# A layer norm's reciprocal deviation moved from GpSimd to ScalarE, with its followers one slot earlier

## The chip, the cores and the metric

One NeuronCore of a Trainium2 chip runs the whole kernel. The metric is the device time of one execution in microseconds; for the kernel before it is 16218.26 us, the median of three runs (16214.16 to 16220.73). Below, PE is TensorE (matmuls), DVE is VectorE, ACT is ScalarE, POOL is GpSimd, and SP is the engine that issues the DMAs.

## The reference, cut to what matters

Two layers work on x of shape (2, 256, 256, 128), fp32, each on a group-normalised input and with a residual. Layer 0 is an attention over rows. Layer 1, which takes nearly all of the time, is a selective scan (a state-space layer) over the L = 65536 pixels of each image, with 256 inner channels and 16 states:

```python
xi, z = split(x @ in_proj_w.T)
xs = silu(depthwise_conv3x3(xi) + conv_b)
dts, Bs, Cs = split(x_proj_w @ xs)
delta = softplus(dt_w @ dts + dt_b)
# for each channel d and state n, along the pixels l:
h[d,n,l] = exp(delta[d,l] * A[d,n]) * h[d,n,l-1] + delta[d,l] * xs[d,l] * Bs[n,l]
y[d,l]   = sum_n h[d,n,l] * Cs[n,l] + Ds[d] * xs[d,l]
mu  = y.mean(over d);  var = ((y - mu)**2).mean(over d)
y   = (y - mu) * rsqrt(var + 1e-5) * ln_g + ln_b
out = x + (y * silu(z)) @ out_proj_w.T
```

The change concerns the rsqrt(var + 1e-5) of the layer norm over the 256 channels, what follows from it, and the sum over n in y.

## The kernel before

**Tiling.** Layer 1 runs in 128 steps (2 images x 64). A step k covers R = 4 image rows, that is T = 1024 pixels. Partitions hold 32 channels times 4 states, so 256 channels and 16 states give 8 x 4 = 32 units a step, each a tile of 128 x 1024. A unit is (k, h, m, q): half h of the channels, group m of states, quarter q of the half.

**The order by hand.** The main loop (from L1041) counts slots t, one unit to a slot, 32 slots to a step; every engine but SP executes its instructions in exactly the order in which the loop emits them. In slot t stand, in this order:

- drive (L951, POOL, odd slots): hb = du * B for the pair of units t+3, t+4, one product of 128x2048
- products (L985, POOL, even slots): h * C for a pooled pair t-2, t-1. Pooled pairs begin at slots 2, 6, 10, 18 and 26 (L588, modulo 32)
- decay (L943, ACT): da = exp(delta * A) of unit t+1, into one of two PSUM tiles
- scan (L964, DVE): the recurrence over the 1024 pixels, from da, hb and the state; for a pooled unit the result goes to hb, otherwise back to da
- product (L976, DVE): h * C into the tile yc, only for units that are not pooled
- y_out (L1024, ACT): copies the finished sum y from PSUM to ys, for the half whose last group of states starts at unit t-8
- the pieces that other parts have put into the slot: those of project, which makes the inputs of a later step (convolution, gates, delta), and those of finish_row, which normalises one image row of an earlier step; first the ones for the other engines, then TensorE's. Within a slot, finish_row's pieces come ahead of project's
- add_up (L998, PE): sums four units over their states into the PSUM tile y, at slot t for units t-6 to t-3. It frees the two yc tiles (of four) that it read
- remember (L971, ACT): the last column of the scan becomes the state

Since ACT keeps this order, a decay can start only after all of the previous slot's ACT pieces and its remember.

**finish_row** (L802) begins at slot a, which is 8, 16, 24 or 0 modulo 32 for the four rows of a step. Its pieces, with their offsets from a before the change: turn (0, PE, y minus its mean, to pixels x channels), stats (1, ACT, squares with a running sum into lss), scales (2, POOL), norm (4, ACT, times rstd), back (5, PE, transposes), gated (6, DVE, yg), mix (7, PE), leave (8, ACT). scales therefore falls on slots 2, 10, 18 and 26, and it is two small GpSimd instructions: lve = lss / 256 + 1e-5 (L838), rstd = lve to the power -1/2 (L839).

**Pieces of project beside it on ACT**, modulo 32: states_out at slots 1 and 2 (L731), size_out at 3, 9, 10 and 11 (L747), softplus at 13 (L755), gate_out at 17, 18, 19 and 27 (L706), silu_z at 21 (L711), normalise at 25 and 26 (L657), silu_xs at 29 (L689). All matmul results of project share one PSUM bank (tag "p"), so each of its matmuls waits until ACT has emptied the last one.

Of the kernel before, what the change touches and what calls it, by code (L numbers as in the profile page):

```python
# [8 lines left out]
F32 = mybir.dt.float32  # L9
AF = mybir.ActivationFunctionType  # L10
ALU = mybir.AluOpType
# [4 lines left out]
P = 128  # L16
GN_EPS = 1e-5
LN_EPS = 1e-5
# [3 lines left out]
def attn_then_ssm_kernel(  # L22
# [26 lines left out]
    nc = tc.nc  # L49
# [4 lines left out]
    DI = in_proj_w.shape[0] // 2  # L54
# [8 lines left out]
    const = ctx.enter_context(tc.tile_pool(name="const", bufs=1))  # L63
# [18 lines left out]
    make_identity(nc, ident)  # L82
    ones_mean = const0.tile([P, P], F32, name="ones_mean")
    nc.vector.memset(ones_mean, 1.0 / P)
    neg_half = const.tile([P, TB // P], F32, name="neg_half")
    nc.vector.memset(neg_half, -0.5)

# [36 lines left out]
    NQ = P // CQ  # L124
    NCG = DI // CQ
    NSG = NS // SR
# [5 lines left out]
    with tc.tile_pool(name="prep", bufs=1) as prep, tc.tile_pool(  # L132
        name="prep2", bufs=3
# [120 lines left out]
    with tc.tile_pool(name="st", bufs=1) as stp, tc.tile_pool(  # L254
        name="st_x", bufs=6
# [20 lines left out]
    with ExitStack() as actx:  # L276
# [242 lines left out]
        end = B * NA  # L519
# [64 lines left out]
    WT = W // P  # L584
# [5 lines left out]
    s2 = ctx.enter_context(tc.tile_pool(name="s2", bufs=2))  # L590
# [14 lines left out]
    def at(t, piece, *args, pe=False):  # L605

        slots.setdefault(t, ([], []))[pe].append((piece, args))
# [194 lines left out]
    def finish_row(k, b, row, t0, a):  # L802
        o = {}

        def fetch():
            o["xres"] = s1.tile([P, WT, C], F32, name="xres")
            nc.sync.dma_start(
                out=o["xres"], in_=x1[b][row].rearrange("(t p) c -> p t c", p=P)
            )
            o["szr"] = s1.tile([P, NH, W], F32, name="szr")  # L810
            nc.sync.dma_start(
                out=o["szr"], in_=given[k]["sz"][:, :, t0 : t0 + W].rearrange("h p t -> p h t")
            )

        def turn():
            o["yt"] = ps_f.tile([P, WT, DI], F32, name="yt", tag="f")
            for j in range(WT):
                for h in range(NH):
                    nc.tensor.matmul(  # L819
                        o["yt"][:, j, :],  # L820
                        ys[k, h][:, t0 + j * P : t0 + (j + 1) * P],
                        centre[:, (1 - h) * P : (1 - h) * P + DI],
                        start=(h == 0),
                        stop=(h == NH - 1),
                    )

        def stats():
            yn = o["yn"] = s1.tile([P, WT, DI], F32, name="yn")
            o["ss"] = s2.tile([P, WT], F32, name="lss")
            for j in range(WT):  # L830
                nc.scalar.activation(  # L831
                    yn[:, j, :], o["yt"][:, j, :], AF.Square, accum_out=o["ss"][:, j : j + 1]
                )

        def scales():
            o["rstd"] = s2.tile([P, WT], F32, name="rstd")
            ve = s2.tile([P, WT], F32, name="lve")
            nc.gpsimd.tensor_scalar(ve, o["ss"], 1.0 / DI, LN_EPS, ALU.mult, ALU.add)  # L838
            nc.gpsimd.tensor_tensor(o["rstd"], ve, neg_half[:, 0:WT], ALU.pow)  # L839

        def norm():
            for j in range(WT):
                nc.scalar.activation(  # L843
                    o["yn"][:, j, :],
                    o["yt"][:, j, :],
                    AF.Copy,
                    scale=o["rstd"][:, j : j + 1],
                )

        def back():  # L850
            o["yd"] = ps_f.tile([P, NH, W], F32, name="yd", tag="f")
            for h in range(NH):
                for j in range(WT):
                    nc.tensor.transpose(  # L854
                        o["yd"][:, h, j * P : (j + 1) * P],
                        o["yn"][:, j, h * P : (h + 1) * P],
                        ident,
                    )

        def gated():  # L860
            o["yg"] = s1.tile([P, NH, W], F32, name="yg")
            nc.vector.tensor_tensor(o["yg"], o["yd"], o["szr"], ALU.mult)  # L862

        def mix():
            o["o"] = ps_f.tile([P, WT, C], F32, name="o1_ps", tag="f")
            nc.tensor.matmul(o["o"], ident, o["xres"], start=True, stop=False)  # L866
            for j in range(WT):
                for h in range(NH):
                    for i, by in enumerate(("yg", "szr")):
                        nc.tensor.matmul(  # L870
                            o["o"][:, j, :],
                            o[by][:, h, j * P : (j + 1) * P],
                            w_out[:, i, h, :],
                            start=False,
                            stop=(j == WT - 1 and h == NH - 1 and i == 1),
                        )

        def leave():
            ob = s1.tile([P, WT, C], F32, name="ob")
            nc.scalar.copy(ob, o["o"])  # L880
            nc.sync.dma_start(
                out=out_tok[b, row * W : (row + 1) * W, :].rearrange("(t p) c -> p t c", p=P),
                in_=ob,
            )

        at(a, fetch)
        for i, piece in (
            (0, turn),
            (1, stats),
            (2, scales),  # L890
            (4, norm),
            (5, back),
            (6, gated),
            (7, mix),
            (8, leave),
        ):
            at(a + i, piece, pe=piece in (turn, back, mix))
# [5 lines left out]
    def unit(t):  # L903

        k, i = divmod(t, NU)
        h, i = divmod(i, NM)
        m, q = divmod(i, NQ)
        return k, h, m, q
# [31 lines left out]
    def pooled(t):  # L940
        return t % NU - t % 2 in POOLED
# [43 lines left out]
    def products(t):  # L985

        k, h, m, q = unit(t)
        hb = units[t]["pair"]
        yc = s4.tile([P, 2, T], F32, name="yc")
        for i in range(2):  # L990
            units[t + i]["yc"] = yc[:, i, :]
        nc.gpsimd.tensor_tensor(  # L992
            yc, hb, repeats["cc", k, h, m].unsqueeze(1).to_broadcast([P, 2, T]), ALU.mult
        )
# [3 lines left out]
    def add_up(t):  # L998

        k, h, m, _ = unit(t)  # L1000
        if m == 0:
            xr = s1.tile([P, T], F32, name="xr")
            nc.sync.dma_start(out=xr, in_=given[k]["xs"][h])
            y = outs["y"] = ps_y.tile([P, T], F32, name="y")
            for i in range(NB):
                cols = slice(i * TB, (i + 1) * TB)
                nc.tensor.matmul(
                    y[:, cols], d_diag[:, h, :], xr[:, cols], start=True, stop=False
                )
        y = outs["y"]  # L1010
        for i in range(NB):
            cols = slice(i * TB, (i + 1) * TB)
            for q in range(NQ):
                nc.tensor.matmul(  # L1014
                    y[q * CQ : (q + 1) * CQ, cols],
                    sel,
                    units[t + q]["yc"][:, cols],
                    start=False,
                    stop=(m == NSG - 1),
                )  # L1020
        for q in range(NQ):
            del units[t + q]

    def y_out(t):  # L1024
        k, h, _, _ = unit(t)
        ys[k, h] = s2.tile([P, T], F32, name=f"ys{h}")
        nc.scalar.copy(ys[k, h], outs["y"])
# [4 lines left out]
    end = len(steps) * NU  # L1032
# [7 lines left out]
    with tc.manual_schedule(engines=engines):  # L1040
        for t in range(min(slots), max(slots) + 1):  # L1041
            if 0 <= t + AHEAD < end:
                fetch(t + AHEAD)
            if 0 <= t < end and t % (NU * NSTEP) == 0:
                st = s1.tile([P, NCG, NSG], F32, name="state")
                nc.gpsimd.memset(st, 0.0)
                states_of[steps[t // NU][0]] = st
            if 0 <= t + 3 < end and t % 2:
                drive(t + 3)
            if 0 <= t - 2 < end and t % 2 == 0 and pooled(t - 2):  # L1050
                products(t - 2)
            if 0 <= t + 1 < end:
                decay(t + 1)
            if 0 <= t < end:
                scan(t)
                if not pooled(t):
                    product(t)
            if 0 <= t - 8 < end and unit(t - 8)[2:] == (NSG - 1, 0):
                y_out(t - 8)
            for pieces in slots.pop(t, ()):  # L1060
                for piece, args in pieces:
                    piece(*args)
            if 0 <= t - 6 < end and (t - 6) % NQ == 0:
                add_up(t - 6)
            if 0 <= t < end:
                remember(t)

# [36 lines left out]
```

## Time and profile before

| what | value | from |
|---|---|---|
| span | 16220.2 us | the page |
| layer 0 and set-up, until the first scans | about 2690 us | the first y sums start at 2697.4 us |
| DVE busy, 4000 to 16000 us | about 96.6% | 1932.80 us in the last 2000 of it |
| POOL busy, same stretch | 97.8% | 1955.10 us |
| ACT busy, same stretch | 68.4% | 1368.25 us |
| PE busy, same stretch | 85.2% | 1703.14 us |
| scan of 128x1024 (DVE) | 2.346 us | the group of L969 |
| product of 128x1024 (DVE) | 1.225 us | the group of L983 |
| decay of 128x1024 (ACT) | 1.117 us | the group of L947 |
| drive or products of 128x2048 (POOL) | 4.54 us | the groups of L957 and L992 |
| lve and rstd (POOL) | 0.191 and 0.689 us | the groups of L838 and L839 |
| table load (ACT) | 1.283 us | the groups of ACT_TABLE_LOAD |

How to read it: busy is the time in which an engine executed something, over a stretch. The busy shares of the whole span mix layer 0 with layer 1, so the stretch from 4000 to 16000 us, which is layer 1 alone, is the one to read. A row of a group gives the line, the engine and operation, the tile written and the tiles read, the shape, the count, the busy time with the mean of one in nanoseconds, and the idle time of that engine just ahead. A row of waits gives who waited for whom, the total in us, how often, and the longest. A row of the timeline gives the start, the duration, the engine, line and operation, and in brackets the idle time before it and what ended it. An ACT_TABLE_LOAD is an instruction of its own on ScalarE: it brings in the table that the next activation function needs.

### The profile page before, as it was taken

The page shows a single profiled execution, that of the slowest core. Times are in us where ns is not written, and L with a number is a line of the kernel's source. Part 1 is how long each engine was busy: PE and PEld are TensorE (multiplying, and loading weights), DVE is VectorE, ACT ScalarE, POOL GpSimd, SP SyncE. Part 2 cuts the span into 40 slices and gives each one's busy share as a digit, 9 for nine tenths or more (in the row PEclk, how much of TensorE's full clock was granted, in tenths as well). Part 3 has the DMA queues.
Part 4 walks back from the last instruction along what each step waited for, and adds up shares of the span by engine and source line. Part 5 has one row for each costly group of instructions (what it writes and reads, how often), then busy time and mean ns, then how long its engine had stood idle before and what let it go on. Part 6 is the DMA issues. An engine that isn't in the chain of part 4 may idle for free. (4 is left out here: it accounts for less than half of the span.)

```text
span 16220.2 us, 178642 instructions
## 1 busy us (share of the span) xinstructions
PE 14005.8 (86%) x59451; PEld 7034.3 (43%) x59451; DVE 14617.8 (90%) x12483; ACT 10627.5 (66%) x18973; POOL 13488.7 (83%) x4240
## 2 busy tenths in 40 slices
PE   6999997888888888888888888888888888888886
PEld 5877883333333333333333333333333333333333
DVE  7665555999999999999999999999999999999998
ACT  3555554666666666666666666666666666666665
POOL 1111114999999999999999999999999999999998
PEclk8999998999999999999999889999999999999998
DMA  4322223666666666666666666666666666666665
GB/s 184 129 95 79 94 79 133 236 235 242 233 234 236 237 236 236 242 234 231 238 235 237 233 234 230 238 235 234 241 233 231 238 234 238 237 240 236 228 239 180
DMA packets 1428911, 3452.16 MB, mean 213 GB/s; under 512 B 119784, under 2 KB 711184, under 8 KB 1407504
## 3 DMA queue, kind: packets, MB, share of 16 engines
q1 hardware_dynamic: 1427984, 3440.73, 59.0%
q8 instruction: 468, 7.67, 0.2%
q14 instruction: 459, 3.76, 0.1%
HBM read 2752.41 MB, written 687.88 MB: 212 GB/s over the span
## 5 line engine op out<-in xcount | busy, mean ns | idle before, releaser
L957 POOL TENSOR_TENSOR hb<-du_r,bb 128x2048 f32<-128x2048 f32 x2048 | 9266.3, 4542 | 71.3 <-DMA du_r<-du_d 15.4
L969 DVE TENSOR_TENSOR_SCAN da<-da,state,hb 128x1024 f32<-128x1024 f32 x2816 | 6607.3, 2346 | 164.7 <-ACT da L947 131.5
L947 ACT ACTIVATE da<-delta_r,a_neg 128x1024 f32<-128x1024 f32 x4096 | 4575.5, 1117 | 84.2 <-DMA delta_r<-delta_d 0.2
L670 PE MATMUL u_ps<-xn,w_tap 128*128 128x512 f32 x9216 | 4230.8, 604 | 7.3 <-ACT sz L706 3.4
L983 DVE TENSOR_TENSOR yc<-da,cc 128x1024 f32<-128x1024 f32 x2816 | 3449.3, 1225 | 423.5 <-PE y L1014 257.4
L969 DVE TENSOR_TENSOR_SCAN hb<-da,state,hb 128x1024 f32<-128x1024 f32 x1280 | 2946.7, 2335 | 15.9 <-ACT da L947 15.9
L992 POOL TENSOR_TENSOR yc<-hb,cc 128x2048 f32<-128x2048 f32 x640 | 2906.7, 4542 | 62.3 <-ACT delta L747 46.8
L670 PEld LDWEIGHTS u_ps<-xn,w_tap 128*128 128x128 f32 x9216 | 1699.1, 194 | 2438.7 <-issue 2003.2
L1014 PE MATMUL y<-yc,sel 128*32 128x512 f32 x16384 | 2562.2, 752 | 14.8 <-POOL yc L992 14.8
L974 ACT COPY state<-da 128x1 f32<-128x1 f32 x2816 | 441.3, 157 | 2838.3 <-DVE yc L983 2797.8
L433 POOL TENSOR_TENSOR x1g<-xc,bo_all 128x512 f32<-128x512 f32 x256 | 315.7, 1272 | 1841.1 <-DVE stats L482 1839.2
L819 PE MATMUL yt<-centre,ys 128*128 128x256 f32 x4096 | 1037.6, 397 | 510.0 <-ACT ob L880 510.0
L695 PE MATMUL z_ps<-xn,w_z 128*128 128x512 f32 x1024 | 801.3, 875 | 696.1 <-ACT sz L706 424.0
L1014 PEld LDWEIGHTS y<-yc,sel 128*32 128x32 f32 x16384 | 492.5, 126 | 1942.6 <-issue 1703.9
L383 ACT ACTIVATE e<-s_ps,nmx 128x256 f32<-128x256 f32 x1024 | 477.0, 475 | 968.6 <-DVE nmx L374 939.9
L819 PEld LDWEIGHTS yt<-centre,ys 128*128 128x128 f32 x4096 | 744.6, 192 | 691.1 <-ACT ob L880 607.6
L736 PE MATMUL dt_ps<-xd,w_dt 8*128 8x512 f32 x1024 | 691.0, 759 | 350.9 <-ACT delta L747 233.2
L870 PE MATMUL o_ps<-w_out,szr 128*128 128x128 f32 x4096 | 797.7, 277 | 0.0
L870 PE MATMUL o_ps<-w_out,yg 128*128 128x128 f32 x4096 | 796.6, 276 | 0.0
L350 DVE TENSOR_TENSOR v<-v_ps,bv_all 128x512 f32<-128x512 f32 x256 | 177.0, 692 | 591.5 <-PE v_ps L343 591.5
L764 POOL TENSOR_TENSOR xs<-delta,xs 128x1024 f32<-128x1024 f32 x256 | 598.7, 2364 | 98.3 <-ACT delta L755 98.3
L870 PEld LDWEIGHTS o_ps<-w_out,yg 128*128 128x128 f32 x4096 | 666.9, 193 | 27.1
(132 smaller groups left out, 16764.6 us busy)
## 6 DMA issues: line engine op xcount, KB each, us to landing
bb<-bc_d SPq DMA_DIRECT2D x1024, 512.0 KB, 4.3
cc<-bc_d SPq DMA_DIRECT2D x1024, 512.0 KB, 4.4
delta_r<-delta_d SPq DMA_DIRECT2D x1024, 512.0 KB, 6.2
du_r<-du_d SPq DMA_DIRECT2D x1024, 512.0 KB, 6.1
sz_d<-sz SPq DMA_DIRECT2D x128, 1024.0 KB, 6.7
szr<-sz_d SPq DMA_DIRECT2D x512, 256.0 KB, 5.6
xs_d<-xs SPq DMA_DIRECT2D x128, 1024.0 KB, 6.6
xr<-xs_d SPq DMA_DIRECT2D x256, 512.0 KB, 5.0
```

Source lines behind the costliest of these rows:

```text
L670: nc.tensor.matmul(o["u"], w_tap[:, h, tap, :], xn[:, i * RB + dy : i * RB + dy + RB, dx : dx + W], start=(tap == 0), stop=(tap == 8),)
L695: nc.tensor.matmul(o["z"], w_z[:, h, :], xn[:, 1 + i * RB : 1 + (i + 1) * RB, 1 : W + 1], start=True, stop=True,)
L736: nc.tensor.matmul(o["dt"], w_dt[:, h, :], o["xd"][0:DR, i * TB : (i + 1) * TB], start=True, stop=True,)
L764: nc.gpsimd.tensor_tensor(du, o["delta"][:, h, :], du, ALU.mult)
L819: nc.tensor.matmul(o["yt"][:, j, :], ys[k, h][:, t0 + j * P : t0 + (j + 1) * P], centre[:, (1 - h) * P : (1 - h) * P + DI], start=(h == 0) ...
L870: nc.tensor.matmul(o["o"][:, j, :], o[by][:, h, j * P : (j + 1) * P], w_out[:, i, h, :], start=False, stop=(j == WT - 1 and h == NH - 1 an ...
L947: nc.scalar.activation(da, spreads["delta", k, h, q], AF.Exp, scale=a_neg[:, g, m : m + 1])
L957: nc.gpsimd.tensor_tensor(hb, spreads["pair", k, h, q], repeats["bb", k, h, m].unsqueeze(1).to_broadcast([P, 2, T]), ALU.mult,)
L969: nc.vector.tensor_tensor_scan(u["h"], u["da"], u["hb"], st, ALU.mult, ALU.add)
L983: nc.vector.tensor_tensor(u["yc"], u["h"], repeats["cc", k, h, m], ALU.mult)
L992: nc.gpsimd.tensor_tensor(yc, hb, repeats["cc", k, h, m].unsqueeze(1).to_broadcast([P, 2, T]), ALU.mult)
L1014: nc.tensor.matmul(y[q * CQ : (q + 1) * CQ, cols], sel, units[t + q]["yc"][:, cols], start=False, stop=(m == NSG - 1),)
```

## The change

The reciprocal deviation is now exp(-1/2 * ln(lss / 256 + 1e-5)), two activations on ScalarE in place of the two instructions on GpSimd. It is for taking the small work off GpSimd, which is nearly always busy, and for keeping the row's statistics on the engine that makes and uses them. Since rstd is then ready within its slot, norm and back come one slot earlier. y's sums come one slot earlier where all four units are DVE's, that is for units 12, 20 and 28 modulo 32; those of units 0, 4, 8, 16 and 24, with a pooled pair among them, stay. The copy of y to ys comes one slot earlier too, from slots 20 and 4 to 19 and 3.

```diff
+    ln_eps = const.tile([P, 1], F32, name="ln_eps")
+    nc.vector.memset(ln_eps, LN_EPS)
...
         def scales():
+            lv = s2.tile([P, WT], F32, name="lve")
+            nc.scalar.activation(lv, o["ss"], AF.Ln, bias=ln_eps, scale=1.0 / DI)
             o["rstd"] = s2.tile([P, WT], F32, name="rstd")
-            ve = s2.tile([P, WT], F32, name="lve")
-            nc.gpsimd.tensor_scalar(ve, o["ss"], 1.0 / DI, LN_EPS, ALU.mult, ALU.add)
-            nc.gpsimd.tensor_tensor(o["rstd"], ve, neg_half[:, 0:WT], ALU.pow)
+            nc.scalar.activation(o["rstd"], lv, AF.Exp, scale=-0.5)
...
-            (4, norm),
-            (5, back),
+            (3, norm),
+            (4, back),
...
-            if 0 <= t - 8 < end and unit(t - 8)[2:] == (NSG - 1, 0):
-                y_out(t - 8)
+            if 0 <= t - 7 < end and unit(t - 7)[2:] == (NSG - 1, 0):
+                y_out(t - 7)
...
-            if 0 <= t - 6 < end and (t - 6) % NQ == 0:
-                add_up(t - 6)
+            for u in (t - 6, t - 5):
+                if 0 <= u < end and u % NQ == 0 and (u == t - 6) == pooled(u + NQ - 1):
+                    add_up(u)
```

## The prediction

> **What bounds the kernel now.** I read the page's busy shares first, then who VectorE waits for in the steady stretch from 4000 to 16000 us, then the rows of one step in order of time.
>
> ```profile
> PE 14005.8 (86%) x59451; PEld 7034.3 (43%) x59451; DVE 14617.8 (90%) x12483; ACT 10627.5 (66%) x18973; POOL 13488.7 (83%) x4240
> ```
>
> DVE and POOL both look like the bound, ACT looks a third idle. In the window, 455 products yg (four to a step) fall in 12000 us: a step of 32 slots takes 12000 / 113.75 = 105.5 us. The waits of DVE there:
>
> ```profile
> DVE yc L983 <- PE y L1014: 232.7, 269, 2.0
> DVE da L969 <- POOL hb L957: 26.8, 88, 1.0
> DVE hb L969 <- ACT da L947: 15.3, 2, 13.3
> DVE yc L983 <- DMA cc<-bc_d: 10.4, 15, 1.7
> ```
>
> The third is two events at the change of image. The other three are 269.9 us, 2.4 us a step: without waits DVE would need 105.5 - 2.4 = **103.1 us a step**. So DVE is the bound, and GpSimd is just behind. I sorted the yc waits by slot (number of the unit modulo 32, found from the pooled pairs, which are scanned into hb): 0.9 us a step at slot 12, 0.3 at slot 20, 0.7 at slot 28, none at 4. A product waits there for a yc buffer that y's sums still read.
>
> The change works in slots 2, 10, 18 and 26, where scales runs. These are first slots of pooled pairs: DVE has two scans and no product. One of them, slots 10 and 11, on DVE and then on ACT:
>
> ```profile
> 10082.74 4.58 DVE L969 TENSOR_TENSOR_SCAN hb<-da,state,hb 128x1024 f32<-128x1024 f32 x2
> 10087.24 2.33 DVE L969 TENSOR_TENSOR_SCAN da<-da,state,hb 128x1024 f32<-128x1024 f32 x1
> ```
>
> ```profile
> 10083.05 1.12 ACT L947 ACTIVATE da<-delta_r,a_neg 128x1024 f32<-128x1024 f32 x1
> 10084.10 0.67 ACT L747 ACTIVATE delta<-dt_ps,dtb_c 128x512 f32<-128x512 f32 x1
> 10085.11 0.19 ACT L974 COPY state<-hb 128x1 f32<-128x1 f32 x1 [0.34 <-DVE hb L969]
> 10085.21 1.11 ACT L947 ACTIVATE da<-delta_r,a_neg 128x1024 f32<-128x1024 f32 x1
> 10086.26 0.67 ACT L747 ACTIVATE delta<-dt_ps,dtb_c 128x512 f32<-128x512 f32 x1
> ```
>
> Call the pair's start S = 10082.74. ACT makes the decay of slot 11 at S+0.31, a piece at S+1.36, and the decay of slot 12 from S+2.47 to S+3.58. DVE needs that one at S+4.50. The margin is **0.9 us**. A mean of 66% hides this; the decay sits in ACT's queue behind everything of its slot. A change of function is dear there:
>
> ```profile
> 10091.11 1.12 ACT L947 ACTIVATE da<-delta_r,a_neg 128x1024 f32<-128x1024 f32 x1
> 10092.25 1.28 ACT L755 ACT_TABLE_LOAD   x1
> 10093.54 1.91 ACT L755 ACTIVATE delta<-delta 128x2048 f32<-128x2048 f32 x1
> 10095.36 0.14 ACT L974 COPY state<-da 128x1 f32<-128x1 f32 x1
> 10095.52 1.28 ACT L947 ACT_TABLE_LOAD   x1
> 10096.81 1.12 ACT L947 ACTIVATE da<-delta_r,a_neg 128x1024 f32<-128x1024 f32 x1
> ```
>
> Softplus costs one load ahead of itself and another ahead of the next Exp. [...]
>
> [...] the load starts 0.02 us after the decay's end and Softplus 0.01 us after the load. [...] The nearest row, a 128x32 Exp of the set-up, took 229 ns. [...] No row of before holds an Ln, so the trace can't say which set this program gets.
>
> **The change part by part.**
>
> *Off GpSimd.* Per row 0.19 us (L838) and 0.69 (L839), and the wait of L838 for ACT: 125.9 us in 455 rows, 0.28 us each. That is 4.6 us a step for POOL. On the end it is worth only what DVE waits for hb, 26.8 us or 0.24 us a step, at slot 20. It is inside the 2.4.
>
> *Onto ScalarE.* Bounds of the loads: none (one set serves Ln and Exp), or two a row (Ln's set, then Exp's again). I take **two**: the loads of before stand directly ahead of the one instruction that finds its function missing[...]. This is a judgement and the largest choice here. ACT's queue in slot 10 is then: decay of 11 ends at S+1.43, load to 2.73, Ln to 3.02, load to 4.31, Exp to 4.50. The next piece starts at S+4.41 (neighbours overlap by 0.09) instead of S+1.36: 3.05 us later. Behind it stand the piece of length X, remember, and the decay of slot 12, which starts X - 0.02 after the piece (0.57 after a piece of 0.59 at another such slot) and takes 1.11. It ends at S+5.50+X. DVE wanted it at S+4.50, so it stalls 1.00+X. X is 0.57 at slot 2 (states_out), 0.67 at 10 (size_out), 0.58 at 18 (gate_out), 0.76 at 26 (normalise): 1.57+1.67+1.58+1.76 = **6.6 us a step**.
>
> *A wait behind it at slot 12.* TensorE's dt_ps of slot 10 waits for the bank that size_out of slot 10 frees, and y's sums of units 4 to 7 stand behind dt_ps; these have a pooled pair, so the diff leaves them there. In a step with S = 10187.61 size_out started at S+1.37 and product 12 got its buffer at S+7.76. With size_out 3.05 us later that is S+10.8. The stalled scan ends S+5.50+0.67, plus 2.42 to the product: S+8.6. Further stall **2.2 us**, which includes the old 0.9. Bounds: 0.9 if the sums catch up, 2.7 if TensorE, idle longer, runs slower still.
>
> *Norm and turning back one slot up, y copied out one slot up.* In slot 3, ACT now holds after its decay (start S+4.96) the copy of y (0.9), norm (0.7), size_out (0.7) and the next decay, ending at about S+9.4. DVE wants that at S+6.1+3.57 = 9.7. Slot 19 is the same with gate_out, 27 and 11 have no copy. I cost it at nothing; scan and product of the next slot hide it.
>
> *Sums of units 12, 20 and 28 one slot up.* They leave the slot in which TensorE is now held up by ACT's late piece, so the waits at slots 20 and 28 (1.0 us a step) go. Also inside the 2.4. The memset of ln_eps runs once: nothing.
>
> *Sum:* 103.1 + 6.6 + 2.2 = 111.9 us a step, 6.4 above 105.5. Times 128 steps: +819 us. **17,040 us**.
>
> **The rivals.**
>
> *One set serves both.* Then scales is two instructions, 0.45 us; the decay of slot 12 ends at about S+4.05 and the margin holds. Waits at 20 and 28 go, slot 12's grows to 0.9+0.45. A step takes 103.1 + 1.35 = 104.45 us: -1.05 x 128, **16,084 us**. [...]
>
> *One load, kept until the next Silu or Softplus.* Those stand in slots 13, 21 and 29, so slots 18, 26 and 2 pay one load. The decay ends at about S+4.2+X, a stall of 0.3 to 0.5, 1.2 a step together: 103.1+1.35+1.2 = 105.65, **16,240 us**, no change.
>
> *GpSimd or spare ScalarE time decides.* If ACT's idle third took the loads and POOL's 4.6 us freed every wait, DVE's floor stays: -2.4 x 128, **15,910 us**. For it: POOL is busy 97.8% of the steady stretch (1955.10 of the 2000 us from 14000). Against it: the 0.9 us margin, and DVE waited for hb only 26.8 us in 12000.
>
> **How the numbers follow.** Two loads a row 0.88, one set 0.07, one load 0.03, DVE's floor 0.02. Within the first: 0.9 at slot 12 and 0.1 us less a row give 110.2 us a step (16,820); 0.3 us more a row, 2.7 at slot 12 and 0.2 lost at slots 5 and 21 each give 114 (17,310). I widen downwards for margins that I took too small: **16,600 to 17,350** leaves out the 0.12 of the rivals and little more. Faster 0.09, same 0.03, slower 0.88.
>
> **What would show it.** 1024 more ACT_TABLE_LOAD, half of them at the Ln's line and half at the rstd Exp's, about 1314 us of ACT. DVE's scans of slots 4, 12, 20 and 28 waiting for ACT's da, some 1.6 us each, where before none did. The yc wait gone at 20 and 28 and about 2 us at 12. POOL with idle time ahead of hb, busy share near 0.9. If there is no load at the Ln beyond the first, the forecast is wrong and the first rival holds; if there are loads but the scans don't wait, my order of ACT's queue is wrong; if the step is near 107, it is the margin that I misjudged.

## The result, and the profile after

The changed kernel takes 17578.1 us in the median (17577.51 to 17579.46) against 16219.45 us of the kernel before in the same runs: **slower by 8.4%**, ratio 1.0838, 95% interval 1.082 to 1.0857. A step of 32 slots takes 116.05 us instead of 105.45 (starts of whole steps in DVE's timeline); 10.6 x 128 = 1357 us is the difference of 1359 us to within 2. The direction was forecast, the size was not: 17,040 us was predicted and 17,350 was the upper end of the range.

The page's busy line:

```profile
PE 14247.4 (81%) x59451; PEld 7239.9 (41%) x59451; DVE 14673.9 (83%) x12484; ACT 12035.8 (68%) x21021; POOL 13080.2 (74%) x3216
```

ACT's share went from 66% to 68%, in a longer span, with 1408 us more of work in it. POOL was relieved and is now idle a quarter of the time, which did not shorten this kernel. The page's shares would let one believe that no engine is the bound.

What ScalarE does at scales, from the groups from 4000 to 17000 us (count, busy us, mean ns):

```profile
L841 ACT ACT_TABLE_LOAD x448 | 574.8, 1283 | 8.1
L839 ACT ACT_TABLE_LOAD x447 | 573.5, 1283 | 8.2
L839 ACT ACTIVATE lve<-lss,ln_eps 128x2 f32<-128x2 f32 x447 | 132.1, 295 | 5.4
L841 ACT ACTIVATE rstd<-lve 128x2 f32<-128x2 f32 x448 | 91.0, 203 | 5.0
```

Two loads a row, one ahead of the Ln and one ahead of the Exp, as taken; the two activations took 0.295 and 0.203 us, 0.50 together. The 0.45 us that the first rival gives them, and their time in the predicted queue, were estimates of mine that no row of before shows; two of the 229 ns of the set-up's Exp are 0.46.

VectorE's waits in the same stretch:

```profile
DVE da L971 <- ACT da L949: 866.2, 448, 2.9
DVE yc L985 <- PE y L1016: 447.2, 218, 2.2
DVE hb L971 <- ACT da L949: 100.3, 114, 7.1
DVE yc L985 <- DMA delta_r<-delta_d: 13.1, 6, 2.2
```

The first line has 448 waits, exactly one for each row of the image: the late decay. The third has about one a step (two in all before): scans of a pooled unit. I sorted the waits by slot as in the prediction, in mean us a step:

| slot | waits for | before | predicted | after |
|---|---|---|---|---|
| 4 | decay (scan) | 0 | 1.57 | 1.64 |
| 8 | y's sums (yc) | 0 | 0 | **1.93** |
| 11 | decay (scan) | 0 | 0 | **0.81** |
| 12 | decay (scan) | 0 | 1.67 | **2.51** |
| 12 | y's sums (yc), DMA | 0.89 | 2.2 | 2.18 |
| 20 | decay, hb, y's sums | 0.60 | 1.58 | 1.65 |
| 28 | decay, y's sums, DMA | 0.84 | 1.76 | 1.93 |
| sum | | 2.3 | 8.8 | 12.65 |

103.1 us without waits and 12.65 us of waits make 115.75 of the 116.05. Three of the four stalls behind the loads are there to within 0.2 us; the waits of slots 8 and 11 and 0.84 us of slot 12's scan were not foreseen.

One pooled pair (slots 2 and 3) of the kernel after, on ACT in order of time:

```profile
10098.38 1.12 ACT L949 ACTIVATE da<-delta_r,a_neg 128x1024 f32<-128x1024 f32 x1
10099.51 1.28 ACT L839 ACT_TABLE_LOAD   x1
10100.81 0.30 ACT L839 ACTIVATE lve<-lss,ln_eps 128x2 f32<-128x2 f32 x1
10101.12 1.28 ACT L841 ACT_TABLE_LOAD   x1
10102.42 0.20 ACT L841 ACTIVATE rstd<-lve 128x2 f32<-128x2 f32 x1
10102.53 0.56 ACT L733 COPY xd<-xd_ps 64x512 f32<-64x512 f32 x1
10102.99 0.19 ACT L976 COPY state<-hb 128x1 f32<-128x1 f32 x1
10103.08 1.11 ACT L949 ACTIVATE da<-delta_r,a_neg 128x1024 f32<-128x1024 f32 x1
10104.14 1.00 ACT L1029 COPY ys<-y 128x1024 f32<-128x1024 f32 x1
10105.04 0.82 ACT L845 ACTIVATE yn<-yt,rstd 128x256 f32<-128x256 f32 x2
10105.76 0.68 ACT L749 ACTIVATE delta<-dt_ps,dtb_c 128x512 f32<-128x512 f32 x1
10106.33 0.19 ACT L976 COPY state<-hb 128x1 f32<-128x1 f32 x1
10106.41 1.13 ACT L949 ACTIVATE da<-delta_r,a_neg 128x1024 f32<-128x1024 f32 x1
```

and the same stretch on DVE, with slot 8 at its end:

```profile
10098.07 4.58 DVE L971 TENSOR_TENSOR_SCAN hb<-da,state,hb 128x1024 f32<-128x1024 f32 x2
10104.29 2.36 DVE L971 TENSOR_TENSOR_SCAN da<-da,state,hb 128x1024 f32<-128x1024 f32 x1 [1.63 <-ACT da L949]
...
10120.53 1.22 DVE L985 TENSOR_TENSOR yc<-da,cc 128x1024 f32<-128x1024 f32 x1 [1.71 <-PE y L1016]
```

The decay that scan 4 needs starts 5.01 us after the pair instead of 2.47 and ends at 6.12; scan 4 waits 1.63 us. That is the predicted chain. The last line is the one that the prediction lacks: product 8 waits for a yc tile that y's sums of units 0 to 3 still read. In the kernel before, the same product had no wait:

```profile
10058.96 4.58 DVE L969 TENSOR_TENSOR_SCAN hb<-da,state,hb 128x1024 f32<-128x1024 f32 x2
...
10078.07 1.22 DVE L983 TENSOR_TENSOR yc<-da,cc 128x1024 f32<-128x1024 f32 x1
```

Why the sums are late is in TensorE's timeline, of the kernel before (pair at 10058.96) and of the kernel after (pair at 10098.07):

```profile
10060.95 1.12 PE L736 MATMUL dt_ps<-xd,w_dt 8*128 8x512 f32 x2 [0.86 <-ACT xd L731]
10062.00 1.92 PE L1014 MATMUL y<-yc,sel 128*32 128x512 f32 x16
10063.86 5.42 PE L670 MATMUL u_ps<-xn,w_tap 128*128 128x512 f32 x12
10069.11 0.60 PE L854 MATMUL yd<-ident,yn 128*128 128x128 f32 x4
10069.55 2.74 PE L670 MATMUL u_ps<-xn,w_tap 128*128 128x512 f32 x6
10072.13 1.88 PE L1007 MATMUL y<-xr,d_diag 128*128 128x512 f32 x4
10073.94 1.92 PE L1014 MATMUL y<-yc,sel 128*32 128x512 f32 x16
```

```profile
10103.14 1.52 PE L738 MATMUL dt_ps<-xd,w_dt 8*128 8x512 f32 x2 [2.06 <-ACT xd L733]
10106.49 4.85 PE L672 MATMUL u_ps<-xn,w_tap 128*128 128x512 f32 x6 [1.83 <-ACT delta L749]
10111.18 0.60 PE L856 MATMUL yd<-ident,yn 128*128 128x128 f32 x4
10111.61 5.32 PE L672 MATMUL u_ps<-xn,w_tap 128*128 128x512 f32 x12
10116.77 1.88 PE L1009 MATMUL y<-xr,d_diag 128*128 128x512 f32 x4
10118.58 1.92 PE L1016 MATMUL y<-yc,sel 128*32 128x512 f32 x16
```

Before, the convolution starts 4.90 us after the pair and the sums end at 16.90. After, it starts at 8.42: it waits for size_out (delta, L749), which now stands behind the loads, the copy of y and norm. And its first six matmuls take 4.85 us, where twelve took 5.42 before: 0.81 us each instead of 0.45. The sums end at 22.43 here; over 14 steps the medians are 16.90 before and 22.68 after, 3.5 us of it from the start and 2.3 from 18 matmuls at 0.58 instead of 0.45 us. Product 8 could start 20.85 us after the pair (scan 8 at 18.43 plus 2.42), so against the median end of the sums it waits 1.8 us. Slot 11 follows, on ACT: leave waits for mix, which stands behind these sums, and all later work of ACT stands behind leave.

```profile
10122.95 0.37 ACT L882 COPY ob<-o_ps 128x256 f32<-128x256 f32 x1 [5.13 <-PE o_ps L872]
...
10127.22 1.12 ACT L949 ACTIVATE da<-delta_r,a_neg 128x1024 f32<-128x1024 f32 x1
```

The second row is the decay of unit 11. It starts 2.0 us after the pooled pair of slot 10 (10125.21); in the pair before the change it was 0.31. So scan 11 waits 0.81 us, and scales of slot 10 starts 1.7 us later than at the other rows.

### The profile page after: what moved, and what is told of

Same layout as the page of the kernel before. It is cut to its first block, busy times and chain, and to the rows that moved or that the text cites. A ratio compares the mean times of both kernels' runs of the same rounds, so it can differ in the third digit from the quotient of the medians.

```text
span 17575.8 us, 179694 instructions
## 1 busy us (share of the span) xinstructions
PE 14247.4 (81%) x59451; PEld 7239.9 (41%) x59451; DVE 14673.9 (83%) x12484; ACT 12035.8 (68%) x21021; POOL 13080.2 (74%) x3216
## 5 line engine op out<-in xcount | busy, mean ns | idle before, releaser
L672 PE MATMUL u_ps<-xn,w_tap 128*128 128x512 f32 x9216 | 4879.3, 681 | 582.4 <-ACT sz L708 302.2
L672 PEld LDWEIGHTS u_ps<-xn,w_tap 128*128 128x128 f32 x9216 | 1952.8, 223 | 3305.4 <-issue 2307.5
L1016 PE MATMUL y<-yc,sel 128*32 128x512 f32 x16384 | 2206.3, 659 | 2.4 <-POOL yc L994 2.4
L697 PE MATMUL z_ps<-xn,w_z 128*128 128x512 f32 x1024 | 685.5, 756 | 891.6 <-ACT sz L708 576.4
L738 PE MATMUL dt_ps<-xd,w_dt 8*128 8x512 f32 x1024 | 737.9, 806 | 801.5 <-ACT delta L749 447.0
L1016 PEld LDWEIGHTS y<-yc,sel 128*32 128x32 f32 x16384 | 451.9, 115 | 1522.6 <-issue 1158.4
L882 ACT COPY ob<-o_ps 128x256 f32<-128x256 f32 x512 | 188.5, 368 | 935.9 <-PE o_ps L872 935.9
L697 PEld LDWEIGHTS z_ps<-xn,w_z 128*128 128x128 f32 x1024 | 188.9, 219 | 1238.3 <-ACT sz L708 797.7
```

The source lines that it names most:

```text
L672: nc.tensor.matmul(o["u"], w_tap[:, h, tap, :], xn[:, i * RB + dy : i * RB + dy + RB, dx : dx + W], start=(tap == 0), stop=(tap == 8),)
L697: nc.tensor.matmul(o["z"], w_z[:, h, :], xn[:, 1 + i * RB : 1 + (i + 1) * RB, 1 : W + 1], start=True, stop=True,)
L738: nc.tensor.matmul(o["dt"], w_dt[:, h, :], o["xd"][0:DR, i * TB : (i + 1) * TB], start=True, stop=True,)
L1016: nc.tensor.matmul(y[q * CQ : (q + 1) * CQ, cols], sel, units[t + q]["yc"][:, cols], start=False, stop=(m == NSG - 1),)
```

## The experiments

Step times and waits by slot are means over the whole steps from 4000 to 16000 us. Before each expectation stands the edit.

**e1: the sums alone.** The kernel before with the last two hunks of the diff.

```diff
+            for u in (t - 6, t - 5):
+                if 0 <= u < end and u % NQ == 0 and (u == t - 6) == pooled(u + NQ - 1):
+                    add_up(u)
```

> The kernel before with one part of the change: y's sums without pooled pairs and the copy of y one slot up; scales stays on GpSimd, norm and back stay. Theory (the waits for yc at slots 20 and 28, 0.34 and 0.73 us a step, were these sums standing behind a late piece of TensorE): both waits gone, slot 12's 0.9 stays, 104.4 us a step, about 16,085 us, ratio 0.992. Rival (GpSimd, busy 97.8%, takes over as the bound at once): the waits for yc turn into waits of the scans for hb, 16,190 to 16,220 us.

16184.91 us, ratio 0.9982 (0.9975 to 0.9989). The yc waits at slots 20 and 28 went, as the theory has it, 1.06 us a step. Half of that came back at once: slot 12 rose from 0.89 to 1.13, scan 11 waits 0.11, hb 0.31 instead of 0.26, a DMA 0.23 instead of 0.11. The rival's range begins 5 us above the result, but not for its reason: the waits for hb rose by only 0.05 us a step. GpSimd did not take over; the gain is small because other waits grew. The part is good for 0.2%.

**e2: Ln and Exp alone.**

```diff
+            nc.scalar.activation(lv, o["ss"], AF.Ln, bias=ln_eps, scale=1.0 / DI)
+            nc.scalar.activation(o["rstd"], lv, AF.Exp, scale=-0.5)
...
             (4, norm),
             (5, back),
```

> The kernel after without its moves: Ln and Exp on ScalarE, but norm, back, y's sums and the copy of y in their old slots. Theory (the loads make the piece behind scales 3 us late, and the sums of slots 18 and 26 stand behind that piece's matmul as those of slot 10 do): new waits for yc at slots 20 and 28 of about 2 us each on top of those of the kernel after, some 120 us a step, about 18,100 us. Rival (the moves are worth nothing when ScalarE is late): as the kernel after, 17,580 us.

18007.24 us, ratio 1.1105 (1.109 to 1.1121), 119.6 us a step. New yc waits at slot 4 (2.17), 20 (1.57) and 28 (1.97): the moves together are worth 430 us once the loads are there. All three new waits are for y's sums, so it is most likely the earlier sums that do it; no run with the loads moves the sums alone. The wait at slot 8 is absent here, against 1.93 in the kernel after: DVE has already lost that time at slot 4.

**e3: one table for both.** The edit, three times, after each Silu and Softplus:

```diff
             nc.scalar.activation(o["xs"], o["xs"], AF.Silu)
+            nc.scalar.preload_act_table_set("natural_log_exp_and_others")
```

> The kernel after, with the table that holds both Ln and Exp loaded right after each Silu and Softplus, in place of the load that the next Exp needs anyway: 3 of these a step as before, none at scales. Theory (the whole loss comes from the 8 loads a step): no scan waits for ScalarE, yc waits only at slot 12 (about 1.3 us), 104.5 us a step, 16,090 us, ratio to the kernel before 0.992. Rival (the order of TensorE's queue, with back in slots 4 and 12 ahead of the convolution, makes the sums of units 0 to 3 late for product 8): 1.9 us a step stay at slot 8, 16,340 us. Rival (two activations and norm are too much for a pooled pair): scans of slots 4, 12, 20 and 28 still wait, over 16,400 us.

16315.88 us, ratio 1.0062 (1.0049 to 1.0075), 106.35 us a step. The loaded table serves both functions: in e12, which has the same edit, Ln (10159.63, 0.28 us) and Exp (10159.94, 0.20 us) follow the decay of 10158.58 with no load ahead of either, and there is none ahead of the next decay (10160.74). The scans of slots 4, 20 and 28 no longer wait at all. So 9.7 of the 10.6 us a step go with the loads. But it is still slower than before: 0.59 us at slot 8, 0.78 at slot 11 and 1.66 at slot 12. The first rival came near in the total and was right only in part on the place: it had 1.9 us at slot 8 and nothing at 11. Without any added load, the moves cost more than they and GpSimd's relief bring.

**e4: scales behind the other pieces of its slot.**

```diff
-            at(a + i, piece, pe=piece in (turn, back, mix))
+            at(a + i, piece, pe=piece in (turn, scales, back, mix))
```

(The second list of a slot is emitted after the first; for an ACT piece it only means later in the queue.)

> The kernel after, with scales behind the other pieces of its slot on ScalarE instead of ahead of them; loads, work and slots are the same. Theory (the yc waits at slots 8 and 12 and the scan waits at slot 11 come from TensorE's matmuls behind a late piece): the scans of slots 4, 12, 20 and 28 still wait 1.6 to 1.9 us, but the yc wait at 8 goes, that at 12 falls to 0 to 1 us, that of the scan at 11 goes and that at 12 falls from 2.5 to 1.7: about 111.3 us a step, 16,970 us. Rival[...]: as the kernel after, 17,580 us.

17576.75 us, ratio 1.0839 (1.0825 to 1.0854): no change in time. The rival's figure was met and the theory's fell, yet the waits did change. The yc wait at slot 12 went (2.07 to 0), as expected of size_out in slot 10. But slot 8 rose from 1.93 to 2.54 and slot 28 from 1.93 to 2.63: size_out of slot 3 is still behind the same things, since decay, copy of y and norm of its own slot stand ahead of it (the convolution starts 8.47 us after the pair in the median, against 8.42). One total can hide two effects; only the sort by slot shows them.

**e5: scales, norm and the copy of y behind.** As e4, with norm too, and y_out emitted after the slot's pieces.

```diff
+            at(a + i, piece, pe=piece in (turn, scales, norm, back, mix))
...
             for pieces in slots.pop(t, ()):
                 for piece, args in pieces:
                     piece(*args)
+            if 0 <= t - 7 < end and unit(t - 7)[2:] == (NSG - 1, 0):
+                y_out(t - 7)
```

> The kernel after with scales, norm and the copy of y behind the other pieces of their slots on ScalarE; the 8 loads a step stay. Theory (what the prediction missed is TensorE's convolution in slots 3 and 19, which waits for size_out or gate_out behind the copy of y and norm, and with it the sums, mix and leave): only the scan waits at slots 4, 12, 20 and 28 stay, 1.6 to 1.9 us each; those at slots 8 and 11 and the yc wait at 12 go: 110.1 us a step, about 16,810 us, below the kernel after by 4.4%. Rival (TensorE is late because ScalarE is 3 us late whatever the order): as the kernel after, 17,580 us, as scales alone behind gave.

17107.48 us, ratio 1.0549 (1.0534 to 1.0565), 112.3 us a step: 471 us less than the kernel after, with the same loads and the same work. Slot 8 fell to 0.04, the yc wait at 12 to 0, slot 11 to 0.45. The stalls of slots 4, 12, 20 and 28 stayed (1.89, 2.68, 1.68, 1.86). From 4000 to 16000 us, first the kernel after, then e5:

```profile
DVE yc L985 <- PE y L1016: 410.2, 200, 2.2
```

```profile
DVE yc L985 <- PE y L1016: 4.3, 7, 0.7
```

The order within the slots is worth 2.9 of the 8.4 points. 16,810 was too low: scan 12 still waits 2.68 and not 1.7 us and scan 11 0.45 and not 0, which is 1.4 of the 2.2 us a step by which it missed.

**e6: one table, norm and the copy of y behind.** e3 with norm in the second list and y_out after the pieces.

```diff
+            at(a + i, piece, pe=piece in (turn, norm, back, mix))
```

> The kernel of the one-table run (16,316 us) with norm and the copy of y behind the other pieces of their slots on ScalarE. Theory (its waits at slots 8 and 11 and the growth at slot 12 come from size_out of slot 3 standing behind them): those go, slot 12 stays at about 1.3: 104.5 us a step, 16,095 us, ratio to the kernel before 0.993. Rival (the convolution is late because the sums that left slot 2 no longer keep TensorE busy ahead of it): 0.6 to 0.8 us at slots 8 and 11 stay, 16,300 us.

16143.3 us, ratio 0.9955 (0.9943 to 0.9967). The waits at slots 8 and 11 went, slot 12 is 1.02; scan 5 now waits 0.60 us for the decay that stands behind the later copy of y. That wait, less what slot 12 fell below its expected 1.3, accounts for most of the 48 us by which the expectation missed. The order alone turned a loss of 0.6% into a gain of 0.45%; back stayed in slot 4, so it was not back that made the sums late. But the theory's word "late" is only half of it:

```profile
10025.30 1.12 PE L740 MATMUL dt_ps<-xd,w_dt 8*128 8x512 f32 x2
10027.20 2.84 PE L672 MATMUL u_ps<-xn,w_tap 128*128 128x512 f32 x6 [0.78 <-ACT delta L751]
```

In this step, as in 74 of 111, the convolution starts 6.5 us after the pair, later than the 5.9 of most steps of e3 (shown under e12). But its gap behind dt_ps is 0.78 us and not 1.86, and its matmuls take 0.45 us and not 0.74. So the order pays here through TensorE's speed more than through the start; e12 tests that.

**e7: one table, only the sums moved.** The edit is against e3.

```diff
-            (3, norm),
-            (4, back),
+            (4, norm),
+            (5, back),
...
-            if 0 <= t - 7 < end and unit(t - 7)[2:] == (NSG - 1, 0):
-                y_out(t - 7)
+            if 0 <= t - 8 < end and unit(t - 8)[2:] == (NSG - 1, 0):
+                y_out(t - 8)
```

> The one-table kernel with norm, back and the copy of y in the slots of the kernel before; only y's sums and scales moved. Theory (norm and the copy of y in slots 3 and 19 made the convolution late): no wait at slots 8 and 11, 1.3 at slot 12, 104.5 us a step, 16,095 us, ratio 0.993. Rival[...]: waits at slots 8 and 11 as in the one-table kernel, 16,300 us.

16138.17 us, ratio 0.9952 (0.994 to 0.9964). No wait at slots 8 and 11; slot 12 is 1.54 and all that is left. Against e3 the earlier norm, back and copy of y cost 178 us, where the prediction costed them at nothing. Against e1, which has scales on GpSimd and the copy of y one slot earlier, e7 is 47 us faster; that is the order of what taking the small work off GpSimd brings when no load is added, though no run shows it by itself.

**e8: sums of units 4 to 7 ahead of dt_ps.** e7, with add_up for these units emitted in slot 10 between the two lists, and no longer at the slot's end.

```diff
+            if 0 <= t - 6 < end and (t - 6) % NU == NQ:
+                add_up(t - 6)
```

> The kernel of the run before this one in the call, with the sums of units 4 to 7 ahead of dt_ps in slot 10 on TensorE instead of behind it. Theory (the wait at slot 12 is these sums standing behind a matmul that waits for ScalarE): it goes and no wait of VectorE is left, 103.2 us a step, 15,930 us, ratio 0.982. Rival (GpSimd's products of that pooled pair come too late, and TensorE waits for them with dt_ps behind it): 1 us or more stays, 16,095 us or above.

16130.06 us, from 16026.74 to 16221.1; ratio 0.9948 (0.9925 to 0.997). The profile is of the slowest of the ten executions (16221.1 us), so it can't stand for the median. In it the wait at slot 12 went, as the theory says, but scans 3 and 13 wait 0.86 and 0.83 us for their decays. The median missed both figures, and neither these two waits nor the spread of 1.2% between the executions was followed to a cause.

**e9: only norm and the copy of y behind, loads kept.** e5 with scales ahead again.

```diff
+            at(a + i, piece, pe=piece in (turn, norm, back, mix))
```

> The kernel after with only norm and the copy of y behind the other pieces of their slots on ScalarE; scales stays ahead, the 8 loads stay. Theory (the step of the prediction that costed the earlier norm and copy of y at nothing is what failed): the waits at slots 8 and 11 go and slot 12's scan wait falls from 2.5 to 1.7, while the yc wait at slot 12 of 2.1, which comes from scales ahead of size_out, stays: 116.05 - 1.93 - 0.81 - 0.8 = 112.5 us a step, 17,120 us, about what was predicted for the whole change. Rival (it was the late states_out and gate_out behind scales): as the kernel after, 17,580 us.

17495.94 us, ratio 1.0788 (1.0772 to 1.0805). The theory fell in its sharp form: 82 us, not 460. In the median the convolution of slot 3 starts at 7.2 us instead of 8.42, but its first matmuls still take 0.89 us each, after an idle time of TensorE of 2.06 us ahead of dt_ps, behind states_out. The sums end at 21.90 instead of 22.68. Slot 8 falls from 1.93 to 0.77, slot 11 stays at 0.74, and slot 21 gains 0.44. With the loads there, both kinds of late piece have to go from ahead of project's (e5); scales alone gives nothing (e4), norm and copy alone little (e9).

**e10: the best of these.** e7 with scales and norm in the second list.

```diff
+            at(a + i, piece, pe=piece in (turn, scales, norm, back, mix))
```

> One table, only y's sums moved, with scales and norm behind the other pieces of their slots. Theory: size_out of slot 10 starts 0.48 us earlier than with scales ahead, so the yc wait at slot 12 falls from 1.5 to about 1.0 us a step: 16,075 us, ratio to the kernel before 0.991. Rival (that wait depends on whether TensorE is at its slower speed and not on 0.5 us): 16,140 us as with scales ahead.

16103.47 us, ratio 0.9929 (0.9916 to 0.9941): faster than both kernels, by 0.7% than before. Slot 12 is 1.05, as expected; scan 4 waits 0.25 us, which was not, and makes up the 28 us between expectation and result.

**e11: the loads alone.** The kernel before with one line.

```diff
             ve = s2.tile([P, WT], F32, name="lve")
+            nc.scalar.preload_act_table_set("natural_log")
```

> The kernel before, with the table that has Ln but not Exp loaded in scales, so that the next decay has to load its own again; the arithmetic stays on GpSimd, nothing is moved. Theory (the loads are the whole loss): as the kernel with Ln and Exp alone (119.6 us a step) less 4 x 0.48 us for the two activations: 117.7 us a step, 17,790 us. Rival (the Ln, the Exp and the wait of one on the other hold ScalarE up): near the kernel before, under 16,500 us.

17020.83 us, ratio 1.0495 (1.048 to 1.0509). VectorE's waits from 4000 to 16000 us:

```profile
DVE da L970 <- ACT da L948: 684.7, 430, 2.6
DVE yc L984 <- PE y L1015: 165.1, 265, 0.8
```

The same arithmetic in the same place, and 1019 loads more (512 at scales, and 887 at the decay where before has 380): 111.6 us a step, 6.2 more than before. So loads that do nothing useful make 800 us, which is neither the theory's figure nor the rival's. They make less than in e2, by more than the two activations take: here the second load stands only ahead of the decay, so project's pieces are 1.3 us late instead of 3.05, and the yc waits stay small (0.17 to 0.73).

**e12: work for TensorE in the gap.** e3, with sums of units 28 to 31 and their copy left where they were.

```diff
+                if 0 <= u < end and u % NQ == 0 and (u == t - 6) == (pooled(u + NQ - 1) or u % NU == NU - NQ):
+                    add_up(u)
```

> The one-table kernel (all moves, no load at scales) with the sums of units 28 to 31 left in slot 2, between dt_ps and the convolution on TensorE, and their copy left in slot 4. The convolution of slot 3 should start when it did, 5.9 us after slot 2, because the sums fill that time. Theory (after a gap of 1.9 us TensorE takes 0.74 us instead of 0.45 for the convolution's next matmuls): 0.45 us each, sums of units 0 to 3 end at 17.9 us instead of 19.6, the waits at slots 8 and 11 go or fall below 0.3 us together: about 105.1 us a step, 16,160 us, ratio to the kernel before 0.996. Rival (the late start alone counts): waits at slots 8 and 11 of 0.6 and 0.8 us as before, 16,316 us.

16190.67 us, ratio 0.9984 (0.9978 to 0.9991). TensorE's timeline, first of e3, then of e12:

```profile
10012.39 1.12 PE L740 MATMUL dt_ps<-xd,w_dt 8*128 8x512 f32 x2
10015.36 4.54 PE L672 MATMUL u_ps<-xn,w_tap 128*128 128x512 f32 x6 [1.86 <-ACT delta L751]
```

```profile
10161.72 3.41 PE L1019 MATMUL y<-yc,sel 128*32 128x512 f32 x16
10165.05 3.01 PE L672 MATMUL u_ps<-xn,w_tap 128*128 128x512 f32 x6
```

The convolution starts later in e12 than in e3 (median 6.29 against 5.90 us after the pair) and yet the sums end earlier (18.29 against 19.56), because a matmul takes 0.47 us and not 0.74. The slow stretch falls on the sums here, which take 3.41 us instead of 1.92. The wait at slot 8 is gone and slot 11 is 0.27, as the theory has it. The rival, that only the start counts, is out. The steps of e3 say the same: in the 86 of 110 whose first six matmuls are slow, product 8 always waits; in the 24 at full speed it never does, though the convolution starts at about 7.1 us in most of these and at 5.9 in most of the slow ones.

## Why the prediction was wrong

- **Two loads a row.** Right: the largest choice, and the one that made the sign. The loads stand at the Ln and at the Exp (447 and 448 in the stretch shown), and without them e3 has no such stall. The placement on which the first rival rested, one table for both, is not what this program got by itself.
- **The stalls of slots 4, 20 and 28**, 1.57, 1.58 and 1.76 us: measured 1.64, 1.65 and 1.93. Right, with the queue as it was laid out.
- **The yc wait of slot 12**, 2.2 us: measured 2.07, and 0.11 for a DMA. Right in its cause, which e4 shows: with scales behind size_out it is gone. The number is helped by luck. Counted from the pair, the product could have started at 10.4 us and not at 8.6, and got its tile at 12.6 and not at 10.8 (medians): both ends of the difference came 1.8 us late.
- **The scan of slot 12**, 1.67 us: measured 2.51. Too small by 0.84. ACT enters slot 10 late by 1.7 us; scan 11's wait takes 0.81 of that, and 0.9 is left. That is arithmetic on the trace: no run with the loads takes this part away (e5 has 2.68).
- **"Norm and turning back one slot up, y copied out one slot up. ... I cost it at nothing; scan and product of the next slot hide it."** This is the step that failed. Its queue was right: it puts the end of size_out in slot 3 at about 8.4 us and of the decay behind it at 9.4, and in the step shown they end at 8.37 and 9.46. I asked of it only whether that decay was in time, and it was: scan 5 and scan 21 have no wait. I did not ask who else waits for size_out in slot 3: the convolution, and behind it on TensorE the sums of units 0 to 3, mix, then leave on ACT, then the decay of slot 11. Before, these sums ended 16.90 us after the pair and product 8 came at 19.11: a margin of 2.2 us that could have been read from the trace as the margin of 0.9 us was. The change makes the convolution 3.5 us late and gives product 8 only 1.7 us more. The moved pieces are not the whole of these 3.5 us. With norm and copy behind, but the loads ahead of states_out, the convolution still starts at about 7.2 us (e9), and only 82 us come back; with the loads gone, the moves cost 178 us (e3 against e7). What was costed at nothing is the lateness of slot 3's queue as a whole, that is loads and moves together.
- **The same step's silence on TensorE's speed.** Slower matmuls stand in the prediction only in the upper bound at slot 12 (in the step that it reads there the 16 sums took 3.63 us, at 10191.70, and those of slot 2 took 1.92, at 10062.00). They add 2.3 us to the end of the sums at slot 8. Without these the sums would end at about 20.4 us (an estimate: 22.68 less 2.3), ahead of the 20.85 at which product 8 is due; e12 shows this without the loads, no run shows it with them.
- **The sum.** 8.8 us of waits predicted, 12.65 measured: slot 8 gives 1.93, slot 11 0.81, slot 12's scan 0.84, the rest 0.3. That is 3.9 us a step, some 490 of the 538 us of the miss. e5 shows that slots 8 and 11 hang on the order of the pieces: with the loads still there it takes 2.25 us of their 2.74 away. The 471 us that e5 gains are not the miss, though: nearly as much, 2.2 us a step, is the yc wait of slot 12, which the prediction had. That no single piece makes the waits of slots 8 and 11 is shown by e4 and e9.
- **Off GpSimd.** Right that it would not decide: POOL is busy 1716.49 of the 2000 us up to 16000, 86%, and in 13000 us it waits 1232.9 us for DVE's scans to free hb. The 0.24 us a step, 31 us, that the prediction allowed for it is of the order of the 47 us of e7 against e1.
- **The first rival's number.** Its 16,084 us for one table was too low as well: e3 took 16,316, for the same omitted step. The nearest is e10 (16,103), where norm and copy are back in their slots and scales and norm stand behind.

## What to carry to other kernels

On an engine that works in order (ACT's thirteen rows under the result stand in the order in which the loop emits them), cost a piece that moves up by asking for every instruction behind it who waits for that one, through the other engines' queues and back, and compare each arrival with its own margin; the nearest deadline is not the only one. A pair of activations two elements wide cost 2.6 us in table loads here: where two functions alternate and one table has both, as in e3 (106.35 us a step against 116.05), load it at the place where a load is due anyway, and read the count of loads in the profile. Where one total does not move, sort the waits by their place in the loop before calling an edit without effect.

## What the runs showed of the hardware

TensorE's matmuls ran at about half their speed after some gaps. The convolution's fp32 matmul of 128x512 took 0.45 us in a full queue and 0.74 to 0.91 us in the first group after gaps of 1.8 to 2.2 us (0.81 in the step shown, with gaps of 2.06 and 1.83 around a short dt_ps); the next group, some 5 us later, was back at 0.44 (5.32 us for twelve). A gap of 0.78 us in e7, after a dt_ps at full speed, left it at 0.45. The trace also holds the clock that TensorE was granted (PEclk, in shares of full speed). In the step shown of the kernel after it is half from 10103.74 to 10110.57 us, over dt_ps and most of the first six matmuls, and full behind that:

```profile
core 0: us, PE busy (x) PEld busy (x) DVE busy (x) ACT busy (x) POOL busy (x), PEclk, DMA share, GB/s
10103.74:10110.57 6.83, 5.00 (x7) 1.85 (x6) 6.16 (x4) 5.07 (x9) 6.75 (x2) 0.50 0.33 120
10110.57:10127.63 17.06, 15.82 (x67) 8.10 (x66) 15.26 (x9) 7.81 (x17) 16.78 (x5) 1.00 0.32 97
```

The length of a gap alone does not settle it. In e3, in slot 19, a longer gap leaves the matmuls at full speed, 2.84 us for six:

```profile
10068.83 2.84 PE L672 MATMUL u_ps<-xn,w_tap 128*128 128x512 f32 x6 [2.26 <-ACT sz L709]
```

In slot 3 of e3 one and the same gap of 1.86 us stands ahead of six matmuls in 4.54 us (at 10015.36) and of six in 2.84 us (at 9273.50). What else decides was not tested. In the step shown the clock was full again 4.1 us after the convolution's start.

A table load took 1283 ns, with next to no idle time of ScalarE around it: the groups shown have 8.1 and 8.2 us of idle time ahead of 448 and 447 loads, 0.02 us each, and 5.4 and 5.0 us ahead of the activations after them, 0.01 us each.
